# Entering a batch by two channel chunks at a time instead of one, at the ends of the scores' rows of block products

## The chip, the cores and the metric

The kernel runs on one core of one Trainium2 chip. The metric is the time of one execution on the device in microseconds; before the change it is 1932.47 us, the median of three runs that lie between 1932.23 and 1932.93 us. The profile is one execution of the same program with the hardware profiler on; its span is 1930.8 us.

## The reference, cut to what matters

Eight images (batches) of 512 channels by 1024 positions, all float32, go through four layers:

```
layer 0: f, g = relu(batchnorm(Wf x)), relu(batchnorm(Wg x)); h = Wh x        # 64 channels each
         z = f^T g (1024 x 1024); attn = z / (largest singular value of z)
         x = Wv (attn applied to h) + bv + x
layer 1: h = groupnorm(x) over 32 groups; q, k, v = Wq h, Wk h, Wv h
         x = x + Wp (softmax(q^T k / sqrt(512)) applied to v)
layer 2: the same with 128 channels, then a batch norm, and x added
layer 3: signs of x times signs of W, scaled, x added, then a leaky ramp
```

The change concerns the last line of layer 0 for one batch: 512 x 1024 outputs whose contraction has 64 terms, the addition to x, and the mean and variance of each channel that layer 1's group norm needs.

## The kernel before, in words

**Layer 0's last line, `enter` (L394 to L438).** The kernel never forms layer 0's 1024 x 1024 matrix. It multiplies small 64 x 64 matrices instead and gets for each batch a weight `pv` (64 x 512, kept in two halves of the partitions; `weights0`, L278) and the map `f` (64 x 1024, its two halves of positions one above the other on the 128 partitions). For each of four channel chunks `oc` of 128, `enter` takes two PSUM banks, multiplies (L403) the upper 64 rows for the first 512 positions and the lower 64 rows for the others, and then VectorE adds each bank, with a bias, to x (L412) and takes its statistics (`bn_stats`, L415). `bn_aggr` (L416) joins the two halves. Each chunk ends with a `yield`, so that the caller decides what stands between chunks. Two more steps follow: a tiny product with `gmat` that averages over groups (L423, which reads what L422 made), and another one (L430), before the scale and bias of the group norm are made.

**Where it is run.** The main loop calls `fast` (L868) once for each batch, in the order 6, 7, 0, 1, 2, 3, 4, 5; numbered n = 0 to 7. While number n's layer-1 scores are made (`scores1`, L506), the one after it is entered, so there are seven entries in the loop. `scores1` has four rows, each of seven block products (a Strassen-like scheme for 2 x 2 blocks; `seven`, L325), so 28 steps, counted by k from 0: a row ends at k = 6, 13, 20, 27. A step is a group of two accumulating 128x128x512 float32 matmuls (L380; a profile shows each float32 matmul as two records). The second, third, sixth and seventh group of a row are read by VectorE (L337), the first, fourth and fifth by ScalarE (L342, L331, L358); GpSimd does one addition (L352). At the end of a row ScalarE takes two exponentials (L521, L522), and VectorE adds them to the running sum (L526, L527) and makes a first difference for the next stage (L567).

Before the change the entry's generator is advanced at k = 12, 15, 18, 21 (one chunk each), 24 and 27 (the two tiny products). For an even batch its first step also makes the weights `pv` of two batches: two matmuls (L282), a copy by ScalarE (L287) and one by VectorE (L285); L403 reads the first.

**The chains.** Layer 0 also needs the largest singular value of each batch. `chain` (L995) squares a matrix again and again, for two batches at once. Each squaring is a pair of 128x128 matmuls (L1008, L1009) whose operand is the copy of the pair before: by ScalarE (L1022), or, every second time, by VectorE (L1030), scaled by the inverse of a trace (L1036, L1037, a tiny matmul L1042, then L1043, L1069, L1070). One pair of batches is finished before the main loop, the other three run behind n = 0, 1 and 2, one step every second k (`chore`).

**What sets the order.** [...] In the main loop a list scheduler orders them when the program is built, from priorities and its own idea of durations; so an edit of where a step stands in the Python moves instructions on all engines. In the main loop all eight PSUM banks are one pool, and a new tile takes a bank that has been released: the first matmul into it waits for the last reader of the tile before. Before the main loop, the first batch (6) is entered by L1433 to L1436, with TensorE's order written out by hand, among the transposes (L1117) and Gram products (L1312) of the later chains and the product of two weights (L1265). There the pool has four single banks and two double ones.

Of the kernel before, what the change touches and what calls it, by code (L numbers as in the profile page):

```python
# [20 lines left out]
CC = C // P  # L21
NT = N // P
HF = 512
NH = N // HF
# [59 lines left out]
def kernel(  # L84
# [17 lines left out]
    nc = tc.nc  # L102
# [18 lines left out]
    def bank():  # L121
        return psum["bank"].tile([P, HF], F32, tag="bank", name="bank")
# [9 lines left out]
    def load_x(b, split=False):  # L132
        t = xpool.tile([P, CC, N], F32, tag="x", name="xt")
        src = x[b].rearrange("(cc p) n -> p cc n", p=P)
        for cc in range(CC):
            for ns in [half(h) for h in range(NH)] if split and not cc else [slice(0, N)]:
                nc.sync.dma_start(out=t[:, cc, ns], in_=src[:, cc, ns])
        return t

    def half(i):  # L140
        return bass.ts(i, HF)

    def side(i):

        return slice(i * MID, (i + 1) * MID)
# [69 lines left out]
    def vec(name):  # L215
        return ct[:, COL[name] : COL[name] + CC]
# [4 lines left out]
    def rsqrt_eps(pool, var, n, name):  # L221

        v = pool.tile([P, n], F32, tag=name + "_v", name=name + "_v")
        r = pool.tile([P, n], F32, tag=name + "_r", name=name + "_r")
        e = pool.tile([P, n], F32, tag=name + "_e", name=name + "_e")
        nc.vector.tensor_scalar(v, var, EPS, None, ALU.add)
        nc.gpsimd.tensor_tensor(r, v, minus_half[:, 0:n], ALU.pow)
        nc.vector.tensor_tensor(e, r, r, ALU.mult)
        nc.vector.tensor_tensor(e, e, v, ALU.mult)
        nc.vector.tensor_scalar(e, e, -0.5, 1.5, ALU.mult, ALU.add)  # L230
        nc.vector.tensor_tensor(r, r, e, ALU.mult)
        return r
# [64 lines left out]
    def quarters_of(t, rows, cols):  # L297

        return [t[:, rows[k], cols[m]] for m in range(2) for k in range(2)]

    def sums_of(a, more, queued=False):

        a11, a12, a21, a22 = a
        s1, s2, s4 = more
        tt = nc.vector.tensor_tensor
        first = tt(s1, a21, a22, ALU.add)
        if queued:
            tc.keep_in_program_order(first)
        tt(s2, s1, a11, ALU.subtract)  # L309
        tt(a21, a11, a21, ALU.subtract)  # L310
        tt(s4, a12, s2, ALU.subtract)
        return {"A11": a11, "A12": a12, "A22": a22, "S1": s1, "S2": s2, "S3": a21, "S4": s4}
# [81 lines left out]
    def enter(xt, f, pv):  # L394

        st = stat.tile([P, CC, NH, 6], F32, tag="st1", name="st1")
        mv = stat.tile([P, CC, 2], F32, tag="mv1", name="mv1")
        for oc in range(CC):  # L400
            banks = [bank() for h in range(NH)]
            for h, ps in enumerate(banks):
                mm(  # L403
                    out=ps,
                    lhsT=pv[side(h), bass.ts(oc, P)],
                    rhs=f[side(h), :],
                    start=True,
                    stop=True,
                )
            for h, ps in enumerate(banks):  # L410
                xs = xt[:, oc, half(h)]
                nc.vector.scalar_tensor_tensor(  # L412
                    xs, ps, bvo[:, oc : oc + 1], xs, ALU.add, ALU.add
                )
                nc.vector.bn_stats(st[:, oc, h, :], xs)  # L415
            nc.vector.bn_aggr(mv[:, oc, :], st[:, oc, :, :])  # L416
            yield

        ps = bank()
        mean = stat.tile([P, CC], F32, tag="mean1", name="mean1")  # L420
        dev = stat.tile([P, CC], F32, tag="dev1", name="dev1")
        nc.vector.tensor_tensor(mv[:, :, 0], mv[:, :, 0], bo, ALU.subtract)  # L422
        mm(out=ps[:, 0:CC], lhsT=gmat, rhs=mv[:, :, 0], start=True, stop=True)  # L423
        nc.vector.tensor_copy(mean, ps[:, 0:CC])
        nc.vector.tensor_tensor(dev, mv[:, :, 0], mean, ALU.subtract)
        nc.vector.tensor_tensor(dev, dev, dev, ALU.mult)
        nc.vector.tensor_tensor(dev, dev, mv[:, :, 1], ALU.add)
        yield
        ps = bank()
        mm(out=ps[:, 0:CC], lhsT=gmat, rhs=dev, start=True, stop=True)  # L430
        sc = rsqrt_eps(stat, ps[:, 0:CC], CC, "r1")
        bi = stat.tile([P, CC], F32, tag="bi1", name="bi1")
        nc.vector.tensor_tensor(sc, sc, vec("L1_conv_gamma"), ALU.mult)
        nc.vector.tensor_tensor(mean, mean, bo, ALU.add)
        nc.vector.tensor_tensor(bi, mean, sc, ALU.mult)
        nc.vector.tensor_tensor(bi, vec("L1_conv_beta"), bi, ALU.subtract)
        norm[:] = sc, bi
        yield  # L438
# [17 lines left out]
    chunks = [slice(0, 2), slice(2, 4)]  # L456
# [49 lines left out]
    def scores1(env, hb, ua, es):  # L506

        scale = float(C) ** -0.5
        esum = env["small"].tile([P, N], F32, tag="esum", name="esum", bufs=1)
        for i in range(NTH):  # L510
            lo, hi = (env["e"].tile([P, N], F32, tag="e", name="e") for _ in range(2))
            es[i], es[NTH + i] = lo, hi
            term = product_of(
                lambda a, b, q, k: hb[b][:, k, bass.ts(i, P)],
                lambda a, b, q, k: ua[a][:, k, :],
            )

            yield from seven(
                term, lo[:, half(0)], hi[:, half(0)], lo[:, half(1)], hi[:, half(1)], exp=scale
            )  # L520
            nc.scalar.activation(lo[:, half(1)], lo[:, half(1)], AF.Exp, scale=scale)  # L521
            nc.scalar.activation(hi, hi, AF.Exp, scale=scale)  # L522
            if i == 0:
                nc.vector.tensor_tensor(esum, lo, hi, ALU.add)
            else:
                nc.vector.tensor_tensor(esum, esum, lo, ALU.add)  # L526
                nc.vector.tensor_tensor(esum, esum, hi, ALU.add)  # L527
        es.append(esum)
# [321 lines left out]
    def entering(n):  # L850

        b = order[n]
        f = load_f(b)

        def steps():
            while b // 2 not in ready:
                next(behind)
            if b % 2 == 0:
                for i in (b, b + 1):
                    pvs[i] = weights0(i)  # L860
            yield from enter(resident[b], f, pvs.pop(b))

        return steps()
# [4 lines left out]
    def fast(env, n, hb, ua):  # L868
# [8 lines left out]
        def chore(every):  # L877
            count[0] += 1
            if count[0] % every == 0:
                next(behind, None)  # L880

        es = [None] * NT
        for k, _ in enumerate(scores1(env, hb, ua, es)):
            if rest3 and k % 2 == 0:
                if next(rest3[0], "end") == "end":
                    rest3.pop()
                    if more and order[n + 1] not in resident:
                        resident[order[n + 1]] = load_x(order[n + 1])
            if n == 0 and k == 2:
                weights["o"] = sums_of(quarters_of(wo, chunks, cols2), [so[:, i] for i in range(3)], True)  # L890
            if n == 0 and k == 6:
                tp = quarters_of(sbw["tpg"], chunks, [slice(0, P), slice(P, 2 * P)])
                weights["tp"] = sums_of(tp, [sp[:, i] for i in range(3)], True)
            if k == 8 and more:
                ahead = entering(n + 1)
            if k >= 11 and k % 3 == 0:
                next(ahead, None)
            if not rest3:
                chore(2)
# [10 lines left out]
        steps = iter(())  # L910
# [6 lines left out]
        if more:  # L917
            steps = make_u(env, hb, got)
# [12 lines left out]
        banks, r = [None, None], None  # L931
# [179 lines left out]
    st = a1.tile([P, 2, B, 6], F32, tag="st", name="st")  # L1111
# [101 lines left out]
    for b in range(B):  # L1213
# [7 lines left out]
        banks = [bank() for _ in w0]  # L1221
# [123 lines left out]
    mv = a1.tile([P, 2, 2], F32, tag="mv", name="mv")  # L1345
# [7 lines left out]
    ps = bank()  # L1353
# [5 lines left out]
    ps = bank()  # L1359
# [65 lines left out]
    with tc.manual_schedule(engines={mybir.EngineType.PE}):  # L1425
        steps = entering(0)
        for k, _ in enumerate(chain(jl, True)):
            for _ in range(2 - k % 2 if k <= 2 * NSTEP else 4):
                next(todo, None)
            for args in (next(relus, None),):  # L1430
                if args:
                    relu(*args)
        for k in range(CC + 2):  # L1433
            next(steps)
            for _ in range(3 if k < CC else 5):
                next(todo, None)  # L1436
        for _ in todo:
            pass
    early.close()
# [52 lines left out]
    def general(env, xt, b, dst):  # L1492
        for _ in enter(xt, load_f(b), weights0(b)):
            pass
# [137 lines left out]
```

## Time and profile before

| what | number |
|---|---|
| median of three runs | 1932.47 us |
| span of the profiled execution | 1930.8 us |
| TensorE busy | 1906.6 us (99%), clock granted 0.998 |
| VectorE busy | 1158.2 us (60%) |
| ScalarE busy | 507.7 us (26%) |
| GpSimd busy | 229.7 us (12%) |
| DMA queue of the loads and stores | 10.0% of 16 engines |

The page lists busy time by engine, the span in 40 slices, the chain of waits that ended last, and the costliest groups of instructions. A timeline lists one engine's instructions in order, equal neighbours merged: start, time from the first start to the last end, the group, how many records, and, in brackets, the idle time before it with what ended it. Matmuls overlap, so their cost is read from one start to the next, not from their durations. VectorE's instructions overlap a little at their ends too, so that the same holds for them.

### The profile page before, as it was taken

Reading aid. Unit: us, or ns where it says so; the run is one execution under the profiler, and the core shown is the slowest. Engines: PE = TensorE matmul, PEld = TensorE weight load, DVE = VectorE, ACT = ScalarE, POOL = GpSimd, SP = SyncE. Lnnn points to the kernel's source line nnn. Section 1 sums busy time; section 2 is a strip of 40 time slices with the busy share of each in tenths; the row PEclk is TensorE's granted clock in tenths of the full one; section 3 lists DMA queues with packets and bytes.
Section 4 is the critical chain, followed back from the end, with each engine's and each line's share of the span. In section 5 each row is a group of like instructions: output and inputs, shape, how many; then the busy total and the mean of one; then the engine's idle time right before and its main releaser. Section 6 shows DMA issues by size and latency. Waiting matters only on the chain.

```text
span 1930.8 us, 16673 instructions
## 1 busy us (share of the span) xinstructions
PE 1906.6 (99%) x6230; PEld 987.4 (51%) x6230; DVE 1158.2 (60%) x1875; ACT 507.7 (26%) x807; POOL 229.7 (12%) x178
## 2 busy tenths in 40 slices
PE   9999999999999999999999999999999999999997
PEld 4367456544655447454555446544645455544653
DVE  3256677448764687537754676348663775466647
ACT  2141222135222332025212331034202421143114
POOL 0000001200111001300121011201120011201121
PEclk9999999999999999999999999999999999999999
DMA  8420000002000120002000120002000200010001
GB/s 319 154 77 7 1 6 12 1 11 87 17 1 0 33 71 12 1 11 87 17 1 1 33 71 11 1 11 87 11 0 1 84 15 11 0 33 22 11 1 46
DMA packets 27784, 66.47 MB, mean 34 GB/s; under 512 B 4272, under 2 KB 5424, under 8 KB 27056
## 3 DMA queue, kind: packets, MB, share of 16 engines
q1 hardware_dynamic: 26768, 64.90, 10.0%
q8 instruction: 51, 0.84, 0.2%
q10 hardware_dynamic: 864, 0.43, 0.1%
q14 instruction: 37, 0.30, 0.1%
q0 software_dynamic: 64, 0.00, 0.0%
HBM read 38.51 MB, written 18.87 MB: 30 GB/s over the span
## 4 chain that ended last, share of the span: by engine, by line
PE 91%; DVE 7%; ACT 1%; issue 1%; DMA 0%; POOL 0%; DVEq 0%; ACTq 0%
PE bank L380 41%; PE bank L547 20%; PE bank L937 6%; PE bank L796 6%; PE bank L1225 4%; PE bank L648 3%; PE bank L403 2%; PE bank L665 2%; PE bank L1008 1%; PE wide L1265 1%; DVE both L739 1%; DVE both L709 1%; PE bank L1009 1%; PE wide L1312 1%; PE bank L688 1%; PE bank L817 1%
## 5 line engine op out<-in xcount | busy, mean ns | idle before, releaser
L547 PE MATMUL bank<-e,vt 128*128 128x512 f32 x768 | 334.0, 593 | 0.0
L547 PEld LDWEIGHTS bank<-e,vt 128*128 128x128 f32 x768 | 145.0, 190 | 175.4 <-issue 173.2
L380 PE MATMUL bank<-ut,h 128*128 128x512 f32 x384 | 181.3, 596 | 0.0
L337 DVE TENSOR_TENSOR e<-bank,e 128x512 f32<-128x512 f32 x128 | 87.6, 684 | 61.1 <-PE bank L380 60.3
L380 PE MATMUL bank<-us,hs 128*128 128x512 f32 x256 | 122.1, 599 | 1.3 <-DVE us L309 0.5
L380 PEld LDWEIGHTS bank<-ut,h 128*128 128x128 f32 x384 | 71.5, 190 | 85.8 <-issue 83.6
L937 PE MATMUL bank<-e,tpg 128*128 128x512 f32 x256 | 114.7, 595 | 0.0
L796 PE MATMUL bank<-tpg 128*128 128x512 f32 x256 | 114.6, 592 | 0.0
L803 ACT ACTIVATE e<-bank 128x512 f32<-128x512 f32 x128 | 76.5, 597 | 128.5 <-PE bank L796 128.5
L352 POOL TENSOR_TENSOR e<-e 128x512 f32<-128x512 f32 x32 | 44.1, 1378 | 419.5 <-ACT e L331 419.5
L380 PE MATMUL bank<-wo,h 128*128 128x256 f32 x384 | 91.8, 382 | 0.0
L808 DVE TENSOR_TENSOR esum<-esum,e 128x1024 f32<-128x1024 f32 x48 | 58.8, 1226 | 54.5 <-ACT e L803 54.5
L380 PE MATMUL bank<-h,wu 128*128 128x512 f32 x192 | 90.3, 593 | 0.7 <-ACT ut L342 0.7
L337 DVE TENSOR_TENSOR vt<-bank,vt 128x512 f32<-128x512 f32 x64 | 44.0, 688 | 70.5 <-PE bank L380 70.0
L937 PEld LDWEIGHTS bank<-e,tpg 128*128 128x128 f32 x256 | 48.1, 190 | 63.2 <-issue 63.1
L796 PEld LDWEIGHTS bank<-tpg 128*128 128x128 f32 x256 | 48.6, 190 | 60.8 <-issue 60.5
L352 POOL TENSOR_TENSOR ut<-ut 128x512 f32<-128x512 f32 x16 | 21.7, 1359 | 478.2 <-ACT ut L333 478.2
L380 PEld LDWEIGHTS bank<-wo,h 128*128 128x128 f32 x384 | 71.6, 190 | 13.5 <-ACT vt L331 4.1
L380 PEld LDWEIGHTS bank<-us,hs 128*128 128x128 f32 x256 | 46.7, 190 | 56.0 <-issue 46.4
L676 ACT ACTIVATE sg<-xt,rb 128x512 f16<-128x512 f32 x64 | 45.0, 718 | 103.7 <-DVE xt L667 100.2
L825 DVE RECIPROCAL rsum<-bank 128x512 f32<-128x512 f32 x15 | 50.3, 3356 | 28.6 <-PE bank L817 28.6
L1225 PE MATMUL bank<-xt,fg 128*64 128x512 f32 x256 | 59.7, 614 | 4.5 <-DMA fg<-in_w_fg 4.5
(325 smaller groups left out, 3090.1 us busy)
## 6 DMA issues: line engine op xcount, KB each, us to landing
xt<-in_x SPq DMA_DIRECT2D x55, 512.0 KB
out<-both SPq DMA_DIRECT2D x63, 256.0 KB
rfull<-rsum SPq DMA_DIRECT2D x60, 128.0 KB
f_dram<-f SPq DMA_DIRECT2D x8, 256.0 KB
fb<-f_dram SPq DMA_DIRECT2D x8, 256.0 KB
w<-in_w SPq DMA_DIRECT2D x1, 1024.0 KB
q<-in_w_q SPq DMA_DIRECT2D x1, 1024.0 KB
k<-in_w_k SPq DMA_DIRECT2D x1, 1024.0 KB
```

The lines of the kernel that those rows point to most:

```text
L337: nc.vector.tensor_tensor(dst, ps, u, ALU.add)
L352: nc.gpsimd.tensor_tensor(c22, c22, c12, ALU.add)
L380: mm(out=ps[:, q * w : (q + 1) * w], lhsT=lt(ka, kb, q, k), rhs=rhs(ka, kb, q, k), start=first and q == 0 and k == 0, stop=last and k == 1 ...
L547: mm(out=ps, lhsT=a[:, t, bass.ts(r_, P)], rhs=e[t], start=first and t == 0, stop=last and t == NTH - 1, skip_group_check=True,)
L648: mm(out=ps[:, i, :], lhsT=xt[:, cc, bass.ts(4 * h + i, P)], rhs=sbw["tpg"][:, cc, 2 * P : 3 * P], start=cc == 0, stop=cc == CC - 1,)
L676: nc.scalar.activation(sg[:, cc, :], xt[:, cc, half(h)], AF.Sign, bias=rb3[:, cc : cc + 1])
L796: mm(out=ps, lhsT=pt[:, 0, bass.ts(t, P)], rhs=tt[:, 0, half(h)], start=True, stop=True,)
L803: nc.scalar.activation(e[:, half(h)], ps, AF.Exp, scale=float(P) ** -0.5)
L808: nc.vector.tensor_tensor(esum, esum, e, ALU.add)
L825: nc.vector.reciprocal(r, ps)
L937: mm(out=banks[h], lhsT=gt[:, t, :], rhs=es[t][:, half(h)], start=t == 0, stop=t == NT - 1,)
L1225: mm(out=banks[i][side(h), :], lhsT=w0[i][:, cc, :], rhs=xt[:, cc, half(h)], start=cc == 0, stop=cc == CC - 1,)
```

## The change

The entry makes two channel chunks in one step: four banks, eight of the L403 records in a row, then the four additions and statistics. The main loop advances it at k = 13 and k = 20, the ends of the second and third row, and then at 24 and 27 as before. The hand-written part before the loop also takes two chunks at a time, with six other pieces of work after each and five after the first tiny product. The aim is to switch TensorE less often between the full array and its halves, and to take the banks where the rows leave most of them free. No arithmetic instruction is added or removed.

```diff
-        for oc in range(CC):
-            banks = [bank() for h in range(NH)]
-            for h, ps in enumerate(banks):
+        for ocs in chunks:
+            banks = [(oc, h, bank()) for oc in range(CC)[ocs] for h in range(NH)]
+            for oc, h, ps in banks:
                 mm(
...
                 )
-            for h, ps in enumerate(banks):
+            for oc, h, ps in banks:
                 xs = xt[:, oc, half(h)]
                 nc.vector.scalar_tensor_tensor(
                     xs, ps, bvo[:, oc : oc + 1], xs, ALU.add, ALU.add
                 )
                 nc.vector.bn_stats(st[:, oc, h, :], xs)
-            nc.vector.bn_aggr(mv[:, oc, :], st[:, oc, :, :])
+                if h:
+                    nc.vector.bn_aggr(mv[:, oc, :], st[:, oc, :, :])
             yield
...
-            if k >= 11 and k % 3 == 0:
+
+            if k in (13, 20, 24, 27):
                 next(ahead, None)
...
-        for k in range(CC + 2):
+        for n in (6, 6, 5):
             next(steps)
-            for _ in range(3 if k < CC else 5):
+            for _ in range(n):
                 next(todo, None)
+        next(steps)
         for _ in todo:
             pass
```

Built, the changed program has, on TensorE, the eight records of L403 in one row at each of these places. VectorE's and ScalarE's instructions are reordered near them too; everything else, GpSimd's order and the transfers included, stands as before. Where two `pv` are made, L282 now stands directly ahead of L403, and ScalarE's copy L287 stands behind the exponential L521 of the row.

## The prediction

> **What bounds the kernel.** I read the page's busy times first, then its chain of waits:
>
> ```profile
> PE 1906.6 (99%) x6230; PEld 987.4 (51%) x6230; DVE 1158.2 (60%) x1875; ACT 507.7 (26%) x807; POOL 229.7 (12%) x178
> PE 91%; DVE 7%; ACT 1%; issue 1%; DMA 0%; POOL 0%; DVEq 0%; ACTq 0%
> ```
>
> TensorE is busy 99% and is 91% of the chain that ended last. So a microsecond in which TensorE waits, or switches its form, is a microsecond of the kernel. VectorE's 60% is a mean. In the stretch of the entry it is another engine: in the table of windows, 247 to 273 us (n = 0), VectorE is busy 22.70 of 26.00 us (87%), TensorE 26.00 of 26.00. Both are nearly full there, and the question is which instruction waits for which.
>
> TensorE's timeline (n = 3) prices an entry's pair of matmuls:
>
> ```profile
> 931.89 1.88 PE L380 MATMUL bank<-ut,hs 128*128 128x512 f32 x4
> 933.61 1.88 PE L380 MATMUL bank<-ut,h 128*128 128x512 f32 x4
> 935.42 1.13 PE L403 MATMUL bank<-fb,pv 64*128 64x512 f32 x4
> 936.48 1.98 PE L380 MATMUL bank<-us,hs 128*128 128x512 f32 x4
> 938.30 1.88 PE L380 MATMUL bank<-ut,h 128*128 128x512 f32 x4
> ...
> 942.30 0.39 PE L423 MATMUL bank<-mv,gmat 128*128 128x4 f32 x2 [0.41 <-DVE mv L422]
> ```
>
> A full group takes 1.72 us from start to start (931.89 to 933.61). Around L403 it is 1.81, then 1.06 for the pair, then 1.82: the pair costs 0.09 + 1.06 + 0.10 = 1.25 us. L423 waits 0.41 us for VectorE.
>
> VectorE's timeline (n = 0) prices its queue:
>
> ```profile
> 270.26 0.75 DVE L412 SCALAR_TENSOR_TENSOR xt<-bank,bvo,xt 128x512 f32<-128x512 f32 x1 [0.16 <-PE bank L403]
> 270.92 1.22 DVE L527 TENSOR_TENSOR esum<-esum,e 128x1024 f32<-128x1024 f32 x1
> 272.06 0.69 DVE L415 BATCH_NORM_STATS2 st<-xt 128x6 f32<-128x512 f32 x1
> 272.66 0.73 DVE L412 SCALAR_TENSOR_TENSOR xt<-bank,bvo,xt 128x512 f32<-128x512 f32 x1
> 273.31 0.15 DVE L1043 COPY tr<-bank 128x1 f32<-128x1 f32 x1
> 273.38 0.68 DVE L337 TENSOR_TENSOR e<-bank,e 128x512 f32<-128x512 f32 x1
> 273.97 0.68 DVE L415 BATCH_NORM_STATS2 st<-xt 128x6 f32<-128x512 f32 x1
> 274.57 0.14 DVE L1069 RECIPROCAL r<-tr 128x1 f32<-128x1 f32 x1
> 274.64 0.67 DVE L567 TENSOR_TENSOR e<-e 128x512 f32<-128x512 f32 x1
> 275.23 0.20 DVE L416 BATCH_NORM_AGGREGATE mv<-st 128x2 f32<-128x12 f32 x1
> ```
>
> Start to start: L412 0.66, L526 or L527 1.13, L415 0.60, L337 0.60, L567 0.59, L416 0.12, the chain's scalars 0.07 each; L1030 takes 0.54 to its end.
>
> [...] no VectorE instruction above starts before its predecessor. So an instruction of the chain standing behind four additions waits for all of them. [...] the trace shows 0.09 and 0.10 us on the two sides of L403. [...] two packed matmuls cost 1.06 us, their two additions with statistics 2 x (0.66 + 0.60) = 2.52 us.
>
> **The change, part by part.**
>
> *Switches saved.* Four matmuls in a row cost 0.09 + 2 x 1.06 + 0.10 = 2.31 us instead of 2 x 1.25 = 2.50. No trace shows four in a row. If the second pair loaded its weights wholly behind the first it would take 0.86 (half a group), if nothing overlapped 1.72; I take 1.06. Saved: 0.19 twice an entry, 0.4 us an entry, at eight entries 3 us. That is the whole gain to be had, apart from one thing: L282 next to L403 saves one exit and one entry, 0.3 us, in n = 1, 3, 5.
>
> *VectorE's work moved into a heap.* Four banks bring 4 x 1.26 + 2 x 0.12 = 5.3 us of VectorE's work at once, at the moment when the row's end brings two L337, L526, L527 and L567 (4.1 us). I walk one place with the built program's order and these prices: n = 0, k = 13, t = 0 at the first L403. TensorE: the four L403 to 2.1; L1008, L1009, L1042 0.7 (as from 270.15 to 270.85 in its timeline); then three groups of the next row, 3 x 1.72 with 0.1 for the tiny ones; at 8.1 it comes to the next L1008, whose operand is L1030's. VectorE: the first pair is complete at 0.53 + 0.59 (last record), so L412 starts at 1.16. In its order follow, up to L1030: L412, L526, L415, two L412, two L415, L416, L412, L1043, L527, L415, L1069, L337, L416, L1070, L567, L1030 = 4 x 0.66 + 2 x 1.13 + 4 x 0.60 + 0.60 + 0.59 + 2 x 0.12 + 3 x 0.07 + 0.54 = 9.5 us. L1030 ends at 10.6. TensorE stands 2.5 us where it did not wait before: all of n = 0 had no idle time on TensorE. Behind L1008 in its queue stands the rest of the row, so nothing fills the gap. n = 2 has the same order: 2.5 us again.
>
> *The next row (k = 20), n = 0, 1, 2.* Same heap. The third group's second half waits for its L337 (VectorE at 10.1, TensorE there at 9.8): 0.3; then L1008 for L1030 (11.4 against 11.0): 0.4. Together 0.7 us each.
>
> *n = 1.* L403 follows L282 at once, and the copy L287 now stands behind L521, which waits for the last L337 of the row. With E the end of the row's last group: L337 ends at E + 0.9, L521 at about E + 1.5, L287 (0.57) at E + 2.1; TensorE was ready at E + 1.1. Wait 1.0 us in place of 0.30. As VectorE does L526 in this wait, L1030 is nearer: 1.7 us instead of 2.5. Sum 1.0 + 1.7 + 0.7 = 3.4, before 0.30 + 0.30.
>
> *n = 3 to 6.* No chain, so the only victim is L423. VectorE passes L422 at 10.7 after the second block (the same heap, one more L337); TensorE arrives at 10.0. Wait 0.75, before 0.41. n = 3 and 5 also have the 1.0 of L287 for 0.30.
>
> *Before the loop.* Here are only four single banks, and the entry takes all. The fourth transpose group (L1117) waits for the fourth L412: from t = 0 at L403 (167.33), VectorE ends it at 173.3, TensorE comes at 171.8: 1.5 us; then L1312 for VectorE's copy, 0.9; then L1265 for the product's copy L1321 behind four additions, 1.3. Followed to L423, it starts at 186.1 instead of 184.44: 1.7 us, with the old wait of 0.61 there gone. Afterwards TensorE has L1265 to do until the normalised batch is ready, as before.
>
> Transfers, GpSimd and statistics cost nothing: their order is unchanged, and the next x is in before k = 13 (DMA share 0.94 from 908 to 912, 0.04 from 912 to 916, L403 at 917.05).
>
> Sum in us: before the loop +1.7; n = 0 and 2: 2.5 + 0.7 - 0.4 = 2.8 each, +5.6; n = 1: 3.4 - 0.6 - 0.4 - 0.3 = +2.1; n = 3 and 5: 0.35 + 0.7 - 0.4 - 0.3 = 0.35 each, +0.7; n = 4 and 6: 0.35 - 0.4, -0.1. Total +10.0: 1932.5 + 10.0 = 1942.5 us.
>
> **Rivals.**
>
> *Only the switches count.* The banks are free at row ends, VectorE empties the heap in time and the old waits for L422 go (4 x 0.41 + 0.61 = 2.25): -3.0 - 0.9 - 2.25 = -6.2, 1926.3 us. For it: VectorE has 3.3 us of slack in 26. Against: the slack lies ahead of the heap, not behind it. 6%.
>
> *Half the waits come.* The waits added are 10.0 + 3.0 + 0.9 = 13.9 us; half leaves 7.0 - 3.9 = +3.1, 1935.6 us, no change that could be told. It would need L1030 about 1.3 us earlier than my walk, which no price above allows, or a slip in one link. 12%.
>
> *The row of four overlaps badly.* The second pair takes 1.72 instead of 1.06: 0.66 x 16 = 10.6 us, of which the waits for VectorE hide about half: 1947.5 us. Against: the two halves of the array overlap fully in each pair now. 8%.
>
> *My forecast*, 74%.
>
> **How the numbers follow.** The range reaches from 1936.4, just above the second rival, to 1947, just below the third; about 2 in 10 lie outside. It takes in the unknown pace of four in a row and 2 us for walks not done in full. Faster by over 0.2% (below 1928.6) is the first rival with a little of the second, 0.06; within 0.2% the second, 0.11; slower, the forecast and the third, 0.83.
>
> **What would show it.** Right: TensorE idle some 2.5 us ahead of L1008 with VectorE's L1030 as releaser, in the middle of the third row, n = 0 and 2; L403 behind L282 waiting 1.0 us for L287; L423 waiting 0.7. L403 with eight records spanning 2.2 us. VectorE without a gap from the first L412 to L1030. Wrong: n = 0 and 2 without idle time, or L1030 done by 8.1 us after L403. What would break the forecast is a shorter price of L412 after L412 than I saw, or a wait satisfied by an earlier instruction than I took.

## The result, and the profile after

The changed kernel takes 1942.7 us, the median of four runs between 1942.55 and 1943.07; the kernel before takes 1932.57 us beside it (1932.23 to 1932.93). The ratio is 1.0053, with a 95% interval from 1.0035 to 1.007: slower by about half a per cent, 10.1 us. The span of the profiled execution goes from 1930.8 to 1941.0 us. In the changed file the lines quoted here stand one or two further down: L1010 and L1011 are the pair of the chain (L1008, L1009), L1032 its copy (L1030), L417 is `bn_aggr`, L424 the tiny product (L423).

The page of the changed kernel, busy times and chain of waits:

```profile
PE 1903.5 (98%) x6230; PEld 989.9 (51%) x6230; DVE 1153.2 (59%) x1875; ACT 508.1 (26%) x807; POOL 228.6 (12%) x178
PE 87%; DVE 11%; issue 2%; ACT 1%; DMA 0%; POOL 0%; DVEq 0%; ACTq 0%
```

TensorE is busy 3.1 us less, and the span is 10.2 us longer. In the chain VectorE has 11% where it had 7%: TensorE now waits for it. Where, TensorE's timeline shows, here around the first block of n = 0, of n = 1 (with its wait for L287) and of n = 2, and the second of n = 3 (a block is the four banks of one step; columns: start, time to the last end, group, records, and in brackets the idle time before it with its releaser):

```profile
251.53 1.99 PE L403 MATMUL bank<-fb,pv 64*128 64x512 f32 x8
253.45 0.49 PE L1010 MATMUL bank<-cur 128*128 128x128 f32 x2
...
257.66 1.88 PE L380 MATMUL bank<-ut,h 128*128 128x512 f32 x4
262.11 0.49 PE L1010 MATMUL bank<-cur 128*128 128x128 f32 x2 [2.57 <-DVE cur L1032]
262.44 0.39 PE L1011 MATMUL bank<-cur 128*128 128x128 f32 x2
262.66 3.08 PE L380 MATMUL bank<-ut,h 128*128 128x512 f32 x4
265.53 2.42 PE L380 MATMUL bank<-us,hs 128*128 128x512 f32 x4
267.79 0.38 PE L1010 MATMUL bank<-cur 128*128 128x128 f32 x2
...
481.89 1.99 PE L403 MATMUL bank<-fb,pv 64*128 64x512 f32 x8 [0.86 <-ACT pv L287]
...
491.41 0.49 PE L1010 MATMUL bank<-cur 128*128 128x128 f32 x2 [1.51 <-DVE cur L1032]
...
718.21 0.49 PE L1010 MATMUL bank<-cur 128*128 128x128 f32 x2 [2.57 <-DVE cur L1032]
...
943.93 1.99 PE L403 MATMUL bank<-fb,pv 64*128 64x512 f32 x8
945.85 1.98 PE L380 MATMUL bank<-ut,h 128*128 128x512 f32 x4
...
954.53 0.39 PE L424 MATMUL bank<-mv,gmat 128*128 128x4 f32 x2 [0.69 <-DVE mv L423]
```

Three things are to be seen. L1010 stands 2.57 us for L1032. The eight records of L403 take 1.92 us to the next start (251.53 to 253.45). And after the wait in n = 0 two groups take 2.87 and 2.26 us from start to start, where a group takes 1.72. VectorE's timeline around the block of n = 0 shows the heap, the work that the block and the row's end bring at once:

```profile
252.70 0.75 DVE L412 SCALAR_TENSOR_TENSOR xt<-bank,bvo,xt 128x512 f32<-128x512 f32 x1 [0.36 <-PE bank L403]
253.36 1.22 DVE L527 TENSOR_TENSOR esum<-esum,e 128x1024 f32<-128x1024 f32 x1
...
258.39 1.21 DVE L528 TENSOR_TENSOR esum<-esum,e 128x1024 f32<-128x1024 f32 x1
259.52 0.69 DVE L415 BATCH_NORM_STATS2 st<-xt 128x6 f32<-128x512 f32 x1
...
260.19 0.67 DVE L337 TENSOR_TENSOR e<-bank,e 128x512 f32<-128x512 f32 x1
...
260.89 0.10 DVE L1072 TENSOR_TENSOR r<-r 128x1 f32<-128x1 f32 x1
260.92 0.68 DVE L568 TENSOR_TENSOR e<-e 128x512 f32<-128x512 f32 x1
261.52 0.54 DVE L1032 TENSOR_SCALAR cur<-bank,r 128x256 f32<-128x256 f32 x1
```

From 252.70 to 262.06 it has no gap, and L1032 is its last piece, 10.5 us after the first L403 (251.53). In the windows from 247 to 273 us TensorE is busy 23.43 of 26.00 us; it was 26.00 before.

The time by stages, from the first scores matmul of a number n to the first of the next stage (the rows of all other stages agree within 0.02 us), and, for the part before the loop, from the first L403 to the first scores matmul:

| stretch | before, us | after, us | difference |
|---|---|---|---|
| before the loop | 53.98 | 55.81 | +1.83 |
| scores n = 0 | 62.06 | 66.67 | +4.61 |
| scores n = 1 | 64.47 | 66.30 | +1.83 |
| scores n = 2 | 62.47 | 65.37 | +2.90 |
| scores n = 3, 5 | 57.86, 57.87 | 57.71, 57.70 | -0.15, -0.17 |
| scores n = 4, 6 | 56.23, 56.24 | 55.72, 55.73 | -0.51, -0.51 |

They sum to 9.83 us. The rest, 0.34 us, lies ahead of the first L403 (167.33 and 167.67), which starts between 165.7 and 167.7 us in the profiled executions of this study (at 167.67 and 167.08 in two executions of the changed kernel), though no edit here touches what stands ahead of it. So two executions may differ by up to two microseconds that belong to no change, and the runs below are compared by stretches too.

### The profile page after: what moved, and what is told of

The parts are those of the page before. It is cut to its first block, busy times and chain, and to the rows that moved or that the text cites. A ratio compares the mean times of both kernels' runs of the same rounds, so it can differ in the third digit from the quotient of the medians.

```text
span 1941.0 us, 16685 instructions
## 1 busy us (share of the span) xinstructions
PE 1903.5 (98%) x6230; PEld 989.9 (51%) x6230; DVE 1153.2 (59%) x1875; ACT 508.1 (26%) x807; POOL 228.6 (12%) x178
## 4 chain that ended last, share of the span: by engine, by line
PE 87%; DVE 11%; issue 2%; ACT 1%; DMA 0%; POOL 0%; DVEq 0%; ACTq 0%
PE bank L380 38%; PE bank L548 20%; PE bank L939 6%; PE bank L797 6%; PE bank L1227 4%; PE bank L649 3%; DVE xt L412 2%; PE bank L666 2%; DVE st L415 1%; PE wide L1267 1%; PE bank L1010 1%; DVE both L740 1%; DVE both L710 1%; PE bank L403 1%; PE bank L1011 1%
## 5 line engine op out<-in xcount | busy, mean ns | idle before, releaser
L337 DVE TENSOR_TENSOR e<-bank,e 128x512 f32<-128x512 f32 x128 | 87.8, 686 | 86.9 <-PE bank L380 86.0
L337 DVE TENSOR_TENSOR vt<-bank,vt 128x512 f32<-128x512 f32 x64 | 44.0, 688 | 70.5 <-PE bank L380 70.0
```

What stands on the lines that cost most here:

```text
L337: nc.vector.tensor_tensor(dst, ps, u, ALU.add)
```

## The experiments

**My theory:** the blocks cost by VectorE's queue. The additions of a block stand ahead of an instruction for which TensorE waits (L1032 for the chain, L423 for the tiny product), and they meet the work of a row's end. **Rivals:** the hand-written part before the loop is what costs; four 64-row pairs in a row, or taking four banks at once, is what costs TensorE.

**1. The loop alone.** The part before the loop is as it was:

```diff
-        steps = entering(0)
+        steps = entering(0, False)     # one chunk at a time
...
-        for n in (6, 6, 5):
+        for k in range(CC + 2):
             next(steps)
-            for _ in range(n):
+            for _ in range(3 if k < CC else 5):
```

> The changed kernel with the part before the main loop as it was (one chunk per step, three other pieces of work after each). My theory: of the 10.2 us that the change adds, 1.8 to 2.2 us come from before the loop (waits of 1.26, 0.82 and 1.25 us there, less what falls away), so 1940.7 us, with the waits of L1010 for L1032 in n = 0 and 2 unchanged at about 2.6 us. Rival, the hand-written part is what costs (its delay is handed on to the whole loop): 1934 us or less. The scores of n = 0 also tell whether the stretch at a granted clock of 0.72 behind the wait comes again: if it belongs to the place, n = 0 lasts 66.7 us again; if it was of that one execution, 65 us.

Measured: 1939.32 us (1939.26 to 1941.86), ratio 1.0043 (1.0026 to 1.006), 1.4 us below the 1940.7 expected. The stretch before the loop is 53.98 us again, so the hand-written part costs its own 1.83 us and no more; that rival has fallen. Of the 3.6 us between the spans of the two profiled executions, 1.6 are the start of the first L403 (166.05 for 167.67). The waits of L1010 are 2.57, 1.51 and 2.57 us as before. But the scores of n = 0, 1, 2 take 64.96, 66.29 and 67.05 us: the slow groups have moved from n = 0 to n = 2. The table of windows of this run says what they are (columns: window, its length, TensorE's busy time and records, granted clock, DMA):

```profile
256.00:259.00 3.00, 0.43 (x4) 1.00 0.00 0
259.00:260.00 1.00, 1.00 (x6) 1.00 0.00 0
260.00:264.00 4.00, 4.00 (x15) 1.00 0.00 0
...
710.00:713.00 3.00, 0.46 (x2) 1.00 0.00 0
713.00:714.00 1.00, 0.97 (x5) 1.00 0.00 0
714.00:718.00 4.00, 4.00 (x7) 0.57 0.00 0
```

After equal waits the clock is 1.00 in n = 0 and 0.57 for 4 us in n = 2. In the changed kernel's own trace it is the other way round: 0.57 from 263 to 267 us in n = 0, 1.00 from 719 to 723 us in n = 2. The last section puts all such waits side by side.

**2. The chain kept out of the heap.** Nothing is left out; the chain only skips its steps around the two blocks:

```diff
-            if not rest3:
+            if not rest3 and k not in (13, 14, 15, 16, 20, 21, 22, 23):
                 chore(2)
```

> The changed kernel, but the chain takes no step at k = 13 to 16 and 20 to 23; the steps left out follow later in the same scores and in the next stage. Nothing is left out of the computation. My theory: the cost is the chain's L1032 standing behind four additions on VectorE while TensorE's queue stands before L1010. Then the waits of 2.57, 1.51 and 2.57 us vanish, and with them the 1.7 us at a lower clock in n = 0 and most of 3 x 0.38: 1933.5 us, the scores of n = 0, 1, 2 at 62 to 64 us; the waits of L424 (0.69 in n = 3 to 6), of L403 for L287 (0.86) and those before the loop stay. Rival, four 64-row matmul pairs in a row or the four banks taken at once are what costs TensorE: no change, 1942 us.

Measured: 1934.92 us (1934.18 to 1935.9), ratio 1.0016 (1.0009 to 1.0023). TensorE's timeline of this run:

```profile
250.99 1.99 PE L403 MATMUL bank<-fb,pv 64*128 64x512 f32 x8
252.91 1.98 PE L380 MATMUL bank<-ut,h 128*128 128x512 f32 x4
...
258.17 1.88 PE L380 MATMUL bank<-us,hs 128*128 128x512 f32 x4
259.88 0.38 PE L1010 MATMUL bank<-cur 128*128 128x128 f32 x2
...
918.50 1.13 PE L282 MATMUL bank<-wv,gm 64*128 64x512 f32 x4
922.25 1.99 PE L403 MATMUL bank<-fb,pv 64*128 64x512 f32 x8 [2.62 <-ACT pv L287]
```

The same block at the same place, with the same 1.92 us, and no wait and no slow group behind it. All three waits for L1032 are gone, and those of 0.38 us in the next row. The rival of the banks and of four in a row has fallen. It came 1.4 us above the 1933.5 expected, which had left out two costs. The skipped steps push the end of the last chain from n = 2 into n = 3 (three pairs of its products stand there now). Its two table loads on ScalarE (1.28 us each) and two scalings on VectorE (0.58 us both) stand there ahead of the row's end, and L403 waits 1.76 us longer for L287: the last line, 2.62 us for 0.86. And L424 now waits 0.68, 0.68 and 0.69 us in n = 0, 1 and 2, where the changed kernel had no such wait.

**3. A shorter heap.** The statistics are taken of the second half of the positions only, so half of them is left out: VectorE has 1.2 us less a block and TensorE the same work:

```diff
-                nc.vector.bn_stats(st[:, oc, h, :], xs)
                 if h:
-                    nc.vector.bn_aggr(mv[:, oc, :], st[:, oc, :, :])
+                    nc.vector.bn_stats(st[:, oc, h, :], xs)
+                    nc.vector.bn_aggr(mv[:, oc, :], st[:, oc, h : h + 1, :])
```

> The changed kernel with the statistics (L415) taken of the second half of the positions only: half of layer 0's statistics for the group norm is left out, TensorE's work is the same. Two chunks then bring VectorE 1.2 us less in a block. My theory: the waits are the tail of VectorE's heap. In n = 0 two statistics (1.2 us) and L568 (0.59) no longer stand ahead of L1032, so L1010 waits 0.8 us in place of 2.57, the same in n = 2, none in n = 1 (1.51), none of L424 for L423 (0.69 each), and shorter waits before the loop: 1933 us. Rival, it is not the length of VectorE's queue but the moment at which the banks or the chain's operand come: the waits stay within 0.5 us, 1941 to 1943 us.

Measured: 1928.87 us (1927.9 to 1929.55), ratio 0.9985 (0.9978 to 0.9992). TensorE's timeline of this run, n = 0 (two rows) and 1:

```profile
255.91 0.49 PE L1010 MATMUL bank<-cur 128*128 128x128 f32 x2 [0.77 <-DVE cur L1032]
...
274.04 0.49 PE L1010 MATMUL bank<-cur 128*128 128x128 f32 x2 [0.63 <-DVE cur L1032]
...
481.61 0.49 PE L1010 MATMUL bank<-cur 128*128 128x128 f32 x2 [0.57 <-DVE cur L1032]
```

0.77 us in place of 2.57, where 0.8 was expected. Ahead of L1032 stand two statistics less (1.2 us), and in this build L568 (0.59 us) stands behind it: 1.8 us of work taken from ahead of L1032 shortens the wait by 1.8 us. L424 waits no more. Two details missed: n = 1 keeps 0.57 us, and the next row has a wait of 0.63 us for L1032 where it had 0.38 for L337. The time is 4.1 us lower than the 1933 expected, partly since the first L403 of this profile starts at 165.66 us, 2.0 us earlier than in the changed kernel.

**4. The blocks in mid-row.**

```diff
-            if k in (13, 20, 24, 27):
+            if k in (10, 17, 24, 27):
                 next(ahead, None)
```

> The changed kernel with its two blocks at k = 10 and 17 in place of 13 and 20: in the middle of the second and third row in place of the ends of the third and... second; the part before the loop as changed. My theory: it is the meeting of the four additions with the row's end (L527, L528, L568 and two L337, 4.1 us on VectorE) that makes the heap too long. In mid-row L1032 ends about 9.0 us after the first L403 and TensorE comes to L1010 at 11.7: no wait, and L424 finds L423 long done: 1930 us, of which about 2 us more than before stem from before the loop. Rival one, two chunks at once are too much anywhere: waits of about 2 us stay, 1940 us. Rival two, in mid-row four banks are not free, and L403 waits for L337's of the row instead: 1 to 2 us in each entry, 1938 us.

(The row ends that this text means are those of the second and third row, k = 13 and 20.) Measured: 1927.23 us (1926.43 to 1928.12), ratio 0.9975 (0.9966 to 0.9984): faster than before, and 2.8 us below the 1930 expected. TensorE's timeline of this run, n = 0 and then n = 1, and last VectorE's L1032 behind the first block:

```profile
245.28 1.99 PE L403 MATMUL bank<-fb,pv 64*128 64x512 f32 x8
...
257.00 0.38 PE L1010 MATMUL bank<-cur 128*128 128x128 f32 x2
...
268.52 0.49 PE L1010 MATMUL bank<-cur 128*128 128x128 f32 x2 [0.40 <-DVE cur L1032]
...
470.58 1.99 PE L403 MATMUL bank<-fb,pv 64*128 64x512 f32 x8 [0.67 <-ACT pv L287]
...
254.29 0.55 DVE L1032 TENSOR_SCALAR cur<-bank,r 128x256 f32<-128x256 f32 x1
```

TensorE comes to the L1010 behind the first block 11.7 us after it (expected 11.7); L1032 ends at 254.84 us, 9.6 us after it (expected 9.0). No wait. L424 finds its operand. In the second block of n = 0, 1, 2 a wait of 0.40 us remains, and 0.67 us for L287 in n = 1, 3, 5. L403 waits for no bank, so the second rival of this run has fallen too: the place at the row's end, chosen for its free banks, was the wrong one, since VectorE's work meets there, and banks in mid-row were free in time.

**5 and 6. The better version, in two steps.** First the mid-row blocks with the part before the loop as it was; then also the weights at a step of their own and the second block one step earlier:

```diff
             if b % 2 == 0:
                 for i in (b, b + 1):
                     pvs[i] = weights0(i)
+            if n:
+                yield
             yield from enter(resident[b], f, pvs.pop(b), two)
...
-            if k in (10, 17, 24, 27):
+            if k in (9, 10, 16, 24, 27):
```

> The blocks of two chunks at k = 10 and 17, and the part before the loop with single chunks as before the change. My theory: the part before the loop costs 1.8 us by its waits alone and nothing of it is handed on, so 1927.2 - 1.8 = 1925.4 us. Rival, the loop's later stages take up such a delay: 1927 us again.

> As the one before, with the weights pv made at a step of their own (k = 9) and the second block at k = 16 in place of 17. My theory: ScalarE's L287 is then over when L403 comes (0.67 us saved in n = 1, 3, 5), and in the built order one VectorE L337 less stands ahead of L1032, which is over at about 7.4 us after the first L403 while TensorE comes at about 8 (0.40 us, and 0.1 for the restart, saved in n = 0, 1, 2): 1925.4 - 2.0 - 1.5 = 1921.9 us. Rival, each wait that goes is replaced by one for a bank, as four are taken at once: 1925 us.

Measured: 1926.02 us (1924.77 to 1926.27), ratio 0.9969 (0.9958 to 0.998), and 1921.33 us (1920.95 to 1922.7), ratio 0.9947 (0.9931 to 0.9964). The stretch before the loop is 53.98 us in both. The page of the last version, and TensorE's timeline around its second block of n = 0, with VectorE's copy for the chain as the last line:

```profile
PE 1898.5 (99%) x6230; PEld 990.5 (52%) x6230; DVE 1160.4 (60%) x1875; ACT 509.1 (27%) x807; POOL 227.7 (12%) x178
PE 92%; DVE 6%; issue 1%; ACT 1%; DMA 0%; POOL 0%; ACTq 0%; DVEq 0%
```

```profile
256.76 1.99 PE L403 MATMUL bank<-fb,pv 64*128 64x512 f32 x8
258.68 1.98 PE L380 MATMUL bank<-us,hs 128*128 128x512 f32 x4
...
262.89 1.88 PE L380 MATMUL bank<-us,h 128*128 128x512 f32 x4
264.60 0.38 PE L1012 MATMUL bank<-cur 128*128 128x128 f32 x2
...
263.71 0.54 DVE L1034 TENSOR_SCALAR cur<-bank,r 128x256 f32<-128x256 f32 x1
```

In the seven scores stages of this run that hold an entry no wait of TensorE reaches 0.25 us, but for one of 0.53 us for L309 at the start of n = 0, which stands in every run here, the kernel before included. The pair of the chain (L1012 in this file) comes 7.8 us after the first L403 of the block, and its operand (L1034) is over at 264.25, 7.5 us after it. By the waits alone, 1921.9 us was expected; no new wait for a bank took the place of one that went.

**7. The kernel before without its own waits.** Single chunks, the weights a step ahead, and the tiny product at k = 25 for n = 3 to 6:

```diff
-            if k >= 11 and k % 3 == 0:
+            if k in (10, 12, 15, 18, 21, 25 if n >= 3 else 24, 27):
                 next(ahead, None)
```

> The kernel before, single chunks, without its own waits: the weights at a step of their own (k = 10) and the tiny product of the means at k = 25 in place of 24 in n = 3 to 6. It tells how much of the gain of the two-chunk versions is in the waits and how much in four L403 in a row. My theory: a block of four costs 2.12 us and two pairs 2 x 1.25 = 2.50, 0.76 us an entry, 5.3 in seven; the waits are 4 x 0.51 + 3 x 0.30 + 0.30 = 3.2 us. So 1931.9 - 3.2 = 1928.7 us. Rival, all the gain of the mid-row version was in the waits: 1926 us or less.

Measured: 1928.05 us (1927.2 to 1928.75), ratio 0.9979 (0.9972 to 0.9986). The scores of n = 4 take 55.56 us here and 54.77 in the version of four banks: 0.79 us an entry. Over the seven scores stages the difference is 5.98 us, where 5.3 were expected (n = 0, 1, 2 differ by 0.93 each, and no run here explains the 0.14 above n = 4). TensorE's busy time says the same, 1904.1 us here and 1898.5 there. So mending the waits brings about 4 us, and the blocks of four another 6.

**8 and 9. The fall of the clock.** The changed kernel once more, and once with each L415 written twice, which gives the same values and 2.4 us more on VectorE in each block:

```diff
                 nc.vector.bn_stats(st[:, oc, h, :], xs)
+                nc.vector.bn_stats(st[:, oc, h, :], xs)
```

> The changed kernel once more, nothing altered. The waits of 2.57 us in n = 0 and n = 2 are alike, but the granted clock fell to a half for about 3.5 us after the first alone in one execution, and after the second alone in another program whose loop is the same and starts 3.5 us earlier. [...] if it is fixed by the program, at n = 0 again. Time 1942 us in any case.

> The changed kernel with each statistic (L415) taken twice: four more of 0.60 us on VectorE in each block, the same values. My theory of the heap: L1032 stands 2.4 us later, so the waits of L1010 become 5.0 us in n = 0 and 2 and 3.9 in n = 1 (2.57 and 1.51), and the waits of L424 about 3 us at most (0.69). For the granted clock: so far it fell to a half after a wait of 2.57 us in three of six cases, in n = 0 or n = 2, and never after 1.51. [...] if the length of the wait isn't what matters, one place again.

Measured: the first 1942.29 us (1941.96 to 1943.11), ratio 1.0055 (1.0038 to 1.0072); in its profile the clock falls in n = 0 again, from about 262.2 to 265.6 us, so the same program showed it twice at the same place. The second 1981.53 us, one run. TensorE's timeline of the second, n = 0, 1 and 2, then its table of windows (columns as above):

```profile
271.96 0.80 PE L1011 MATMUL bank<-cur 128*128 128x128 f32 x2 [4.95 <-DVE cur L1033]
295.13 1.98 PE L380 MATMUL bank<-ut,hs 128*128 128x512 f32 x4 [2.77 <-DVE e L337]
...
507.35 0.49 PE L1011 MATMUL bank<-cur 128*128 128x128 f32 x2 [3.88 <-DVE cur L1033]
...
741.57 0.79 PE L1011 MATMUL bank<-cur 128*128 128x128 f32 x2 [4.94 <-DVE cur L1033]
```

```profile
268.00:272.00 4.00, 0.04 (x1) 0.67 0.00 0
272.00:276.00 4.00, 4.00 (x8) 0.50 0.00 0
...
508.00:512.00 4.00, 4.00 (x7) 0.57 0.00 0
...
741.00:747.00 6.00, 5.43 (x10) 0.50 0.00 0
```

The waits are 4.95, 3.88 and 4.94 us, where 5.0, 3.9 and 5.0 were expected: four statistics of 0.60 us give 2.4 us more, in all three places. The run is 39 us longer than the changed kernel, 8.0 us of it before the loop and 28.5 in the seven scores stages, since other waits come too, such as the 2.77 us for L337 in the next row. In n = 3 to 6 L424 (here L425) waits 0.48 us only, but the second tiny product behind it 1.93, for L429 on VectorE. The clock falls in all three places, in the first and last already during the wait and for about 6.8 us. Before the loop there are two more long waits in this run, of 3.40 and 3.62 us, and the clock falls after both, for 3.4 us.

## Why the prediction was right, and where its terms were not

The time was forecast at 1942.5 us and is 1942.7, by the mechanism named. But two terms were off in opposite directions: the entries in the loop save 2.7 us more than forecast, and the fall of the clock costs 1.7 us that the forecast does not have. The rest of the balance is 0.3 us ahead of the first L403, 0.1 before the loop, and some 0.5 us in each of n = 0 and 2, of which the restarts after two stops (below) are about 0.2 and the remainder stays open. That all this nearly cancels is luck.

- **The heap on VectorE** was right step by step. L1032 was to end 10.6 us after the first L403 and ends at 10.5; the wait was to be 2.5 us and is 2.57 in n = 0 and 2. Runs 3 and 9 confirm it as a sum: 1.8 us less work ahead of it, 1.8 us less wait, 2.4 more work, 2.4 more wait. n = 1 was to wait 1.7 us and waits 1.51; L287 1.0 and 0.86; L424 0.75 and 0.69. Run 2 shows that it is the chain that suffers. One reading was not right, though nothing rests on it: n = 0 was not wholly without idle time before, TensorE waits 0.53 us there for L309 (at 223.72 us), ahead of the entry, and does so after the change too.
- **The order on VectorE**, on which this rested, is to be seen in the trace after: the bank that the chain's copy L1045 reads is filled at 254.28 us (the end of L1044 on TensorE), and L1045 starts at 258.32, behind additions, statistics and L527. L1032's scale L1072 is over at 260.99 us, and L568, for which nobody on TensorE waits, still runs first, 0.60 us.
- **The next row** was to cost 0.7 us each in n = 0, 1, 2: 0.3 for L337 and 0.4 for L1030. The first shows as 0.38 us; the second is no idle time above 0.25, but L1010 starts 0.23 us late there (at 738.13 in n = 2; the two records ahead of it start at 736.94 and take 0.53 and 0.43). A stop also costs about 0.1 us more than its idle time: the next group's first step takes 0.53 us in place of 0.43.
- **Before the loop** +1.7 was forecast and +1.83 measured, by waits of 1.26, 0.82 and 1.25 us (1.5, 0.9 and 1.3 in the prediction), and L424 waits no more there.
- **The step that was mis-sized** is "I take 1.06" for the second pair of a block, with bounds of 0.86 and 1.72. It is the lower bound. Call one record on each half of the array, side by side, a pass: inside a block the passes follow at 0.53, then 0.43 and 0.43 us, so a block costs 0.09 + 1.06 + 0.86 + 0.10 = 2.11 us, not 2.31. The eight records span 1.99 us, not 2.2. A block saves 0.39 us, not 0.19; an entry saves 0.78, not 0.4; seven entries 2.7 us more than forecast. That is why n = 4 and 6 gain 0.51 us where 0.05 was forecast: -0.78 + (0.69 - 0.41) = -0.50. The 0.09 and 0.10 us on the two sides of L403 are paid once for two pairs in a row: the group ahead takes 1.81 us (249.72 to 251.53 in n = 0), the group behind 1.82 (945.85 to 947.67 in n = 3), and the step from pair to pair is 0.43.
- **The term that was missing** is the clock. Where it falls, the scores last 1.7 us longer: n = 0 +4.61 against n = 2 +2.90 for the same waits, and run 1 with the two exchanged; 0.43 x 4 us lost in a window at 0.57 is 1.72 us.
- **The rivals.** "Only the switches count" needed VectorE to empty the heap in time; it has no gap until L1032 is over, and TensorE stands. "Half the waits" needed L1030 1.3 us earlier; it came 0.1 earlier. "The row of four overlaps badly" has the opposite sign of what was measured. I wrote that the switches were "the whole gain to be had", 3 us: run 7 against run 6 shows 6 us.

## What to carry to other kernels

Collecting work on the busiest engine into larger pieces also delivers its consumers' work in larger pieces. Walk the queue of the engine that empties them up to the next instruction for which the first engine waits, and set the piece where that queue is short, not where the buffers are free: here the blocks at the ends of rows, with two chunks at a time before the loop as well, cost 10 us; three or four steps earlier, with the weights made a step ahead and the part before the loop left alone, they gained 11 (1921.3 against 1932.1 us). And look at what stands in that queue without a consumer in a hurry, like L568 here.

## What was not expected of the hardware

**A wait of a few microseconds can cost TensorE more than its length, and its length alone does not decide.** After some waits the granted clock was a half for about 3.4 us (a window of 4 us at 0.57 is 3.44 us at a half). After the waits of 4.95 and 4.94 us it was a half for about 6.8 us, twice that. It followed all five waits between 3.40 and 4.95 us, three of ten between 2.57 and 2.77 us, and none of 1.51 (three) or 1.93 us (four).

When the clock fell is worked out from the granted clock of windows of 0.5 or 1 us:

| wait | us | clock falls | at 0.50 for, us |
|---|---|---|---|
| changed kernel, n = 0 | 2.57 | 1.1 us after its end | 3.4 |
| changed kernel, n = 2 | 2.57 | no | - |
| once more (run 8), n = 0 | 2.57 | 0.7 us after its end | 3.4 |
| once more (run 8), n = 2 | 2.57 | no | - |
| run 1, n = 0 | 2.57 | no | - |
| run 1, n = 2 | 2.57 | 1.3 us after its end | 3.4 |
| run 2, n = 3 | 2.62 | no | - |
| run 9, L337 in n = 0 | 2.77 | no | - |
| run 9, L337 in n = 1 | 2.75 | no | - |
| run 9, L337 in n = 2 | 2.75 | no | - |
| run 9, before the loop | 3.40 | 0.4 us after its end | 3.4 |
| run 9, before the loop | 3.62 | 1.0 us after its end | 3.4 |
| run 9, n = 1 | 3.88 | 0.9 us after its end | 3.4 |
| run 9, n = 0 | 4.95 | 2.3 us after its start | 6.8 |
| run 9, n = 2 | 4.94 | 3.8 us after its start | 6.8 |

The wait of 2.57 us stands at the same two places of the same loop in the first six rows. Two profiles of the changed kernel have the fall in n = 0, and run 1, in which L1010 starts 3.5 us earlier in n = 0 (258.65 for 262.11) and 5.2 us earlier in n = 2 (713.03 for 718.21), has it in n = 2. So neither the length of the wait nor its place in the program fixes whether the clock falls. That the moment at which the wait comes has a part in it fits these six rows, but no run moved a wait in time and nothing else, and what decides was not shown. The waits are the profile's, in which the ends of matmuls are modelled.

**Four packed passes in a row** cost 2.11 us and not twice 1.25: the second pair follows at 0.43 us a pass, the pace of a record of the full array (1.72 us for the four of a group).
